# Cross keys of two sequences in one pass, and a new order of round 0, in a fused decoder layer

## The chip, the cores and the metric

The kernel runs on one core of one Trainium2 chip. The metric is device time in microseconds; three runs of the kernel before took 3400.95, 3402.79 and 3403.72 us, and the median, 3402.79, is the time before. A core has five engines that run side by side, each in the order of its own queue: TensorE (PE in the profile, its weight loads PEld), VectorE (DVE), ScalarE (ACT), GpSimd (POOL) and SyncE (SP), which here only issues DMAs.

## The reference

One decoder layer over 32 sequences of 256 tokens with 256 features, in f32: self-attention with a latent of 72 (16 heads), cross-attention with 16 heads of 64 to a context of 120 rows, and a mixture of 16 experts that each choose 32 tokens of a sequence, with a shared expert beside them. A layernorm follows each part.

```python
# self-attention: one latent serves as keys and as values of all heads
Wdkv = x @ latent_w + latent_b
q = jnp.einsum('btc,hcl->bhtl', x, Wd_w) + Wd_b[None, :, None, :]
scores = jnp.einsum('bhtl,bsl->bhts', q, Wdkv) / np.sqrt(d_head)      # causal mask
y = jnp.einsum('bhts,bsl->bhtl', softmax(scores), Wdkv)
x = _layernorm(x + y_of_all_heads @ out_w + out_b)
# cross-attention: keys and values come from the context alone
k = jnp.einsum('bsd,dhk->bshk', ctx, Wk)
v = jnp.einsum('bsd,dhk->bshk', ctx, Wv)
logits = jnp.einsum('bthk,bfhk->bhft', k, q * depth ** -0.5)
x = _layernorm(x + einsum(softmax(logits), v) @ Wo)
# experts: the 32 best tokens of each expert and sequence
scores = jax.nn.softmax(x @ gate_w.T, axis=-1).transpose(0, 2, 1)
topk_w, topk_idx = jax.lax.top_k(scores, 32)
x = _layernorm(x + scattered(expert(x[topk_idx]) * topk_w) + shared(x))
```

## The kernel before

The kernel has two stages. In the first, which takes about two thirds of the time, a round n (a first and a second half) does the self-attention of sequence n, and beside it later steps of earlier sequences: the self-attention's end and the cross queries of n-1, the cross-attention of n-1 and n-2, and turn_x2, routing and selection of n-3. In the second stage the experts run, one after the other, over 16 sequences each.

The order of TensorE and ACT is written out by hand: the calls in `first_half` and `second_half` are their queues, round after round. In round 0 SP's order is by hand too, and in the opening, up to the call of `load_weights([(wk_sb, wk)])` (lines 959 to 975), that of all engines. In the other rounds a scheduler places the work of VectorE, POOL and SP; it honours `urgent()`, which raises the priority of the copies that empty PSUM. The kernel uses eight banks of PSUM, six of them in one rotation (tag "r"): a step that takes a bank waits until its tenant of six steps ago was copied out.

The steps that matter here:

- `keys` (L342) makes kT on ACT and kD on VectorE from xT. `place_keys` sends kT to kr by four DMAs. `queries(s, g)` (L388) makes the queries of four heads, with eight passes of TensorE over 256 columns and a pair of copies on ACT. `query_rest` makes q8 for the last eight latent columns of all heads. `scores(s, g)` (L416) needs kr, q8, kT, kD and the queries, fills four banks, and VectorE adds the mask.
- `weights(s, g, t)` is the softmax of one block: VectorE takes the maximum, ACT does four exponentials with their sums, VectorE the reciprocals and POOL the product (L471). `turns(s, g)` transposes the result on TensorE (pT), and ACT and VectorE copy it to pt. `weigh`, `weigh_rest` and `latent_out` finish the self-attention, which gives x1; `turn_x1` transposes x1 and VectorE copies the result to x1T, which `cross_queries` needs.
- `load_context(s)` (L330) loads the context of one sequence. `cross_keys(s, n)` (L557) makes one half of its keys: four chunks of 128 features, each with two weight blocks of 128 by 128 against the 120 context rows, into one bank (pkx), and a copy on ACT to kxT. `cross_values` (L571) makes half of the values, pvx to vx. `cross_scores`, `cross_weights` (xsm on ACT, L463, and rs_x on VectorE), `cross_turn` (pxT to xpt), `cross_weigh` and `cross_out` finish the cross-attention.
- In the opening `first_weights` issues the first loads, `order_first` brings the first query weights into order on VectorE (wd_sb, after wdbs), `order_others` the rest on VectorE and POOL. `warm_up(n)` runs n matmuls on a unit matrix whose result nobody reads.
- `select(g)` transposes the scores of eight sequences and copies them to `left`; `choose(g, k)`, for k from 0 to 3, finds the next eight best on VectorE (max, its indices, and a replacement of what was found); `place(g)` turns the indices for the gathers. Select comes at the end of rounds 10, 18 and 26, and `best_of` calls the choose steps in the next round.

Of the kernel before, what the change touches and what calls it, by code (L numbers as in the profile page):

```python
# [32 lines left out]
def decoder_kernel(  # L33
# [208 lines left out]
    def first_weights():  # L242


        nc.sync.dma_start(
            out=lat_sb[:, :, 0:L], in_=latent_w.rearrange("(c p) l -> p c l", p=P)
        )
        by_part = wd_w.rearrange("(c p) n -> p c n", p=P)
        for part in (slice(0, HG * L), slice(HG * L, H * L)):
            nc.sync.dma_start(out=raw[:, :, part], in_=by_part[:, :, part])  # L250
        nc.scalar.dma_start(out=latb[0:L], in_=latent_b.unsqueeze(1))
        for j in range(1, HG):
            nc.scalar.dma_start(
                out=latb[LM + j * LR : LM + (j + 1) * LR], in_=latent_b[LM:].unsqueeze(1)
            )
        nc.scalar.dma_start(out=wdb_sb, in_=wd_b)

        nc.scalar.activation(warm, mhalf[:, 0:1], AF.Exp)
        by_column = wd_b[LM:, :].rearrange("l (g j o) -> j (l g) o", j=HG, o=1)
        for j in range(HG):  # L260
            nc.sync.dma_start(
                out=wdbs[j * 32 : (j + 1) * 32, ZC - 1 : ZC], in_=by_column[j]
            )
        nc.vector.tensor_copy(
            lat_sb[:, :, L:].rearrange("p c (j l) -> p c j l", l=LR),
            lat_sb[:, :, LM:L].unsqueeze(2).to_broadcast([P, DC, HG - 1, LR]),
        )
        nc.sync.dma_start(out=outb, in_=out_b.partition_broadcast(P))

    def pack(copy, g):  # L270
# [46 lines left out]


    states = [{} for _ in range(B)]

# [6 lines left out]
        st["x"] = sp.tile([P, TC, C], F32, tag="x", name=f"x_{s}")  # L327
        nc.sync.dma_start(out=st["x"], in_=x[s].rearrange("(t p) d -> p t d", p=P))

    def load_context(s):  # L330
        st = states[s]
        st["c"] = ap.tile([P, DC, S2], F32, tag="c", bufs=3, name=f"c_{s}")
        nc.sync.dma_start(out=st["c"], in_=ctxT[s].rearrange("(c p) s -> p c s", p=P))

    def turn_x(s):
        st = states[s]
# [217 lines left out]

    def cross_keys(s, n):  # L557
        st = states[s]
        if n == 0:
            st["kxT"] = ap.tile([P, QC, S2], F32, tag="kxT", name=f"kxT_{st['nm']}")  # L560
        pkx = bank("r", [P, 4, S2], f"pkx_{st['nm']}_{n}")
        for c in range(4):
            w0 = (4 * n + c) * P
            project(
                pkx[:, c, :],
                [(wk_sb[:, d, w0 : w0 + P], st["c"][:, d, :]) for d in range(DC)],
            )
        with urgent():
            nc.scalar.copy(st["kxT"][:, 4 * n : 4 * n + 4, :], pkx)

    def cross_values(s, n):  # L571
        st = states[s]
        if n == 0:
            st["vx"] = ap.tile([S2, H, DH], F32, tag="vx", bufs=2, name=f"vx_{st['nm']}")
        pvx = bank("r", [S2, 512], f"pvx_{st['nm']}_{n}")
        project(
            pvx,
            [(st["c"][:, d, :], wv_sb[:, d, n * 512 : (n + 1) * 512]) for d in range(DC)],
        )
# [25 lines left out]
    def cross_scores(s, c0, t):  # L605
        st = states[s]
        nm = f"{st['nm']}_{c0}_{t}"
        pLs = [bank("l", [P, HG, S2], f"pL_{nm}_{odd}") for odd in range(2)]
        for j in range(HG):
            for odd in range(2):  # L610
                rows = slice(odd * DH, (odd + 1) * DH)
                nc.tensor.matmul(  # L612
                    pLs[odd][:, j, :],
                    st["qxT", c0][rows, j, t * P : (t + 1) * P],
                    st["kxT"][rows, c0 + j, :],
                    start=True,
                    stop=True,
                )
        st["pL", c0, t] = pLs
# [127 lines left out]
    def select(g):  # L747

        sc = scs[g]
        pst = bank("r", [P, T], f"pst_{g}")  # L750
        for t in range(TC):
            nc.tensor.transpose(
                pst[:, t * P : (t + 1) * P], sc[:, t].rearrange("p b e -> p (b e)"), ident
            )
        left = ap.tile([P, T], F32, tag="left", bufs=1, name=f"left_{g}")
        with urgent():
            nc.vector.tensor_copy(left, pst)
        idx = ap.tile([P, CAP], mybir.dt.uint32, tag="idx", bufs=1, name=f"idx_{g}")
        ats[g] = left, idx
        choose(g, 0)  # L760

    def choose(g, k):

# [46 lines left out]
    def first_half(n):  # L810
        scores(n, 0)
        run(cross_scores, n - 2, 4, 0)
        run(cross_values, n - 1, 0)
        turns(n - 1, 3)
        both(cross_turn, n - 2, 0, 1)
        both(cross_weights, n - 2, 4, 0)
        queries(n, 1)
        if n == 0:
            turn_x(1)
            keys(1)  # L820
        run(turn_x2, n - 3)
        weights(n, 0, 0)
# [4 lines left out]
            route((n - 3) // BQ)  # L827
        run(cross_weigh, n - 2, 0)
        weights(n, 0, 1)
        best_of(n, 1)  # L830

        scores(n, 1)
        run(cross_scores, n - 2, 4, 1)
        run(latent_out, n - 1)
        if n:
            run(load, n + 1)
            run(load_context, n + 1)
        else:
# [12 lines left out]
        run(cross_weights, n - 2, 4, 1, 1)  # L851
        if n == 0:
            out_weights(0)
        if routed(n):
            score((n - 3) // BQ)
        run(turn_x1, n - 1)
        run(cross_values, n - 1, 1)
        run(cross_queries, n - 1, 0, 0)
        run(cross_queries, n - 1, 0, 2)
        best_of(n, 2)  # L860

    def second_half(n):
# [19 lines left out]
        best_of(n, 3)  # L882

        weigh(n, 0)
        weigh(n, 1)
# [29 lines left out]
    def last_scores():  # L915
# [8 lines left out]
        weights(last, 2, 1)  # L924
        queries(last, 3)
        both(cross_weights, last - 1, 0, 0)
        cross_keys(last, 1)
        scores(last, 3)
        cross_scores(last - 1, 0, 1)
        both(cross_weights, last - 1, 0, 1)  # L930
# [249 lines left out]
    with tc.manual_schedule(engines=pinned):  # L1180
# [43 lines left out]
        score(last // BQ)  # L1224
        fill(3)
        select(B // BG - 1)
        for k in range(1, CAP // 8):
            choose(B // BG - 1, k)
        fill(8)
        place(B // BG - 1)  # L1230
# [54 lines left out]
```

## Time and profile before

| what | value |
|---|---|
| median of three runs | 3402.79 us |
| the profiled execution | 3404.24 us |
| its span, first to last instruction | 3402.5 us |
| VectorE, ACT, POOL busy | 1534.1, 1503.1, 1071.8 us |
| passes over the cross keys (pkx) | 1024 of 128x120 |
| copies to kxT on ACT | 64 of 128x480, median 587 ns |
| passes over the cross values (pvx) | 256 of 120x512 |
| step of a round in the middle of the first stage | 72.96 us (round 3 to 4, from transposes at 211.09 to 284.05) |

The span counts from the first to the last instruction of the profiled execution; what lies around it is 1.7 us. A matmul of f32 data shows in the trace as two passes. Passes are pipelined: the length of a single one (say 274 ns) reaches beyond the start of the next, so a pass's cost is the step from one start to the next, which one reads from a group's length in the chain of waits. An arrow in the column of idle time names what ended a wait.

### The profile page before, as it was taken

What the parts mean: (1) busy time and instruction counts of PE and PEld (TensorE: products, weight loads), DVE (VectorE), ACT (ScalarE), POOL (GpSimd) and SP (SyncE); (2) the same over time, 40 slices, a digit from 0 to 9 for tenths busy, and PEclk for the clock granted to TensorE, in tenths of its full rate; (3) what the DMA queues carried; (4) which work ended last, traced back from release to release, by engine and by line L of the source; (5) the groups of instructions that cost most, each with busy time, mean ns of one, the idle gap of its engine ahead of it and who ended that gap; (6) DMA issues with size and microseconds to landing.
All of it is one profiled execution on the core that took longest, in us unless ns stands there. A gap on an engine that the chain in (4) does not pass through costs nothing.

```text
span 3402.5 us, 60296 instructions
## 1 busy us (share of the span) xinstructions
PE 3379.7 (99%) x23544; PEld 2574.4 (76%) x23544; DVE 1534.1 (45%) x3416; ACT 1503.1 (44%) x5461; POOL 1071.8 (31%) x947
## 2 busy tenths in 40 slices
PE   9999999999999999999999999999999999999999
PEld 7888888888888888888888888887666655666655
DVE  4555555555555555555555555554312133211133
ACT  4655555555555555555555555554311111111111
POOL 3333332323232323233233233233444401444400
PEclk9999999999999999999999999999999999999999
DMA  3000000000000000000000000003455531555421
GB/s 99 9 17 23 20 21 18 18 18 23 20 17 22 17 18 18 26 17 20 19 18 17 24 20 20 17 12 102 112 122 122 137 90 57 124 123 122 105 86 47
DMA packets 142883, 164.56 MB, mean 48 GB/s; under 512 B 29448, under 2 KB 118536, under 8 KB 142600
## 3 DMA queue, kind: packets, MB, share of 16 engines
q1 hardware_dynamic: 117808, 126.08, 12.4%
q0 software_dynamic: 24576, 34.62, 5.8%
q8 instruction: 187, 3.06, 0.4%
q14 instruction: 96, 0.79, 0.1%
q10 hardware_dynamic: 216, 0.01, 0.0%
HBM read 105.61 MB, written 50.86 MB: 46 GB/s over the span
## 4 chain that ended last, share of the span: by engine, by line
PE 97%; DVE 1%; ACT 1%; POOL 0%; DMA 0%; issue 0%; POOLq 0%; ACTq 0%
PE po L188 14%; PE pq L188 7%; PE pqx L188 7%; PE pd L188 6%; PE pu L188 6%; PE pg L188 6%; PE pS L438 5%; PE pz L505 5%; PE pT L485 5%; PE pc L654 3%; PE pL L612 3%; PE pkx L188 3%; PE pu_s L188 3%; PE pg_s L188 3%; PE pxT L638 3%; PE pfo L188 3%
## 5 line engine op out<-in xcount | busy, mean ns | idle before, releaser
L471 POOL TENSOR_TENSOR sm<-sm,rs 128x512 f32<-128x512 f32 (+1 forms) x256 | 375.8, 1468 | 457.3 <-DVE rs L470 443.0
L463 ACT ACTIVATE sm<-sm,nmax 128x128 f32<-128x128 f32 (+1 forms) x1024 | 453.5, 462 | 89.5 <-DVE nmax L460 89.5
L471 POOL TENSOR_TENSOR xsm_x<-xsm_x,rs_x 128x480 f32<-128x480 f32 x256 | 252.5, 988 | 733.2 <-DVE rs_x L470 731.2
L463 ACT ACTIVATE xsm_x<-pL,nmax_x 128x120 f32<-128x120 f32 x1024 | 355.6, 378 | 10.5 <-DVE mv L160 7.7
L1059 POOL DMA_INDIRECT acc<-eo,offs x128 | 200.8, 1569 | 335.7 <-DVE eo L1056 294.6
L447 DVE TENSOR_TENSOR sm<-pS,mask 128x384 f32<-128x384 f32 x512 | 248.9, 547 | 90.7 <-PE pS L438 90.6
L188 PE MATMUL pq<-xT,wd_sb 128*128 128x256 f32 x1152 | 279.4, 384 | 0.6 <-DVE wdbs L290 0.6
L188 PE MATMUL po<-ow_sb,zT 128*128 128x256 f32 x1152 | 257.2, 382 | 0.0
L188 PE MATMUL pg<-xeT,wg 128*128 128x512 f32 x512 | 240.8, 593 | 0.0
L188 PE MATMUL pu<-xeT,wu 128*128 128x512 f32 x512 | 240.7, 592 | 0.0
L188 PEld LDWEIGHTS po<-ow_sb,zT 128*128 128x128 f32 x1152 | 216.2, 190 | 31.9
L188 PE MATMUL pqx<-x1T,wq_sb 128*128 128x256 f32 x1024 | 239.7, 382 | 0.0
L1130 DVE TENSOR_TENSOR hT<-gl,pu 128x512 f32<-128x512 f32 x128 | 87.9, 688 | 333.4 <-PE pu L188 199.4
L188 PEld LDWEIGHTS pq<-xT,wd_sb 128*128 128x128 f32 x1152 | 212.2, 191 | 30.5 <-DVE wdbs L290 0.7
L460 DVE TENSOR_REDUCE nmax<-sm 128x4 f32<-128x512 f32 (+1 forms) x256 | 231.4, 945 | 2.3
L463 ACT ACTIVATION_READ_ACCUMULATOR xsm_x<-pL,nmax_x 128x1 f32 x1024 | 229.1, 224 | 0.0
L188 PE MATMUL po<-wo_sb,cxT 128*128 128x256 f32 x1024 | 227.6, 380 | 0.0
L188 PE MATMUL pd<-wd,hT 128*128 128x256 f32 x1024 | 226.6, 379 | 0.0
L188 PEld LDWEIGHTS pqx<-x1T,wq_sb 128*128 128x128 f32 x1024 | 189.6, 190 | 40.7 <-issue 13.6
L470 DVE RECIPROCAL rs<-rs 128x4 f32<-128x4 f32 x256 | 45.5, 178 | 378.1 <-ACT sm L463 374.8
L463 ACT ACTIVATION_READ_ACCUMULATOR sm<-sm,nmax 128x1 f32 x1024 | 211.7, 207 | 0.0
L188 PEld LDWEIGHTS pd<-wd,hT 128*128 128x128 f32 x1024 | 192.1, 190 | 25.7 <-issue 1.0
(139 smaller groups left out, 6075.8 us busy)
## 6 DMA issues: line engine op xcount, KB each, us to landing
wg<-in_wg_dram SPq DMA_DIRECT2D x32, 512.0 KB
wu<-in_wu_dram SPq DMA_DIRECT2D x32, 512.0 KB
wd<-in_wd_dram SPq DMA_DIRECT2D x32, 512.0 KB
x<-in_x_dram SPq DMA_DIRECT2D x32, 256.0 KB
rows<-x SPq DMA_DIRECT2D x32, 256.0 KB
acc<-x SPq DMA_DIRECT2D x32, 256.0 KB
x2t<-x2T SPq DMA_DIRECT2D x32, 256.0 KB
fx2T_s<-x2t SPq DMA_DIRECT2D x16, 512.0 KB
```

The lines of the kernel that those rows point to most:

```text
L188: nc.tensor.matmul(acc, lhsT, rhs, start=(i == 0), stop=(i == n - 1))
L438: nc.tensor.matmul(pS[2 * a + odd][:, SEG[t]], st["qT", g][rows, a, t * P : (t + 1) * P], k[rows, 0 : (t + 1) * P], start=False, stop=(t = ...
L447: nc.vector.tensor_tensor(sm[:, j, :], pS[j], mask, ALU.add)
L460: nc.vector.tensor_reduce(nmax, src, AX.X, ALU.max, negate=True)
L463: nc.scalar.activation(dst[:, a, :], src[:, a, :], AF.Exp, bias=nmax[:, a : a + 1], accum_out=rs[:, a, :],)
L471: nc.gpsimd.tensor_tensor(dst, dst, rs.to_broadcast([P, n, width]), ALU.mult)
L485: nc.tensor.transpose(pT[:, j, :], block, ident)
L505: nc.tensor.matmul(pz[odd * LM : (odd + 1) * LM, a, k * P :], st["v"][:, k, 0:LM], moving(st, g, 2 * a + odd, k), start=(k == 0), stop=(k ...
L612: nc.tensor.matmul(pLs[odd][:, j, :], st["qxT", c0][rows, j, t * P : (t + 1) * P], st["kxT"][rows, c0 + j, :], start=True, stop=True,)
L638: nc.tensor.transpose(pT[:, j, :], st["xsm", c0, t, odd][:, j, :], ident)
L654: nc.tensor.matmul(pc[odd * DH : (odd + 1) * DH, a, :], st["vx"][:, 2 * (c0 + j0 + a) + odd, :], st["xpt", c0, odd][:, j0 + a, :], start=True,
L1059: nc.gpsimd.indirect_dma_start(out=acc[b], out_offset=self.rows(b), in_=eo[:, k, :], in_offset=None, compute_op=ALU.add,)
```

## The change

1. `cross_keys` works on a pair of sequences. A context tile holds both sequences side by side, so each weight block meets 240 columns in one pass. A half of the keys now takes two banks of two chunks, and two copies to kxT. The tile of the keys is one for each half, with one buffer each, in place of two buffers for the whole. Pairs from the second on do this in odd rounds: the first half of the keys in the first half of the round, the second in the second. In even rounds `cross_keys` is left out. Pair 0 is done in round 0.
2. `load_context` loads a pair, by two DMAs, in even rounds, in place of one sequence in each round.
3. In the opening `order_first` comes ahead of `keys(0)`, the first queries directly behind the first keys, `warm_up(6)` goes, and the context loads move behind `wk`. `load(1)` moves ahead of `outb`.
4. In rounds 0 and 1 `queries(0, 2)`, `queries(0, 3)` and `queries(1, 1)` stand earlier, and the pair's keys stand where `queries(0, 2)` stood.
5. In every round `both(cross_turn, n - 2, 4, 0)` moves from ahead of `queries(n, 2)` to behind `turn_x1`. In even rounds `cross_values(n - 1, 1)` takes the place that `cross_keys` leaves, ahead of `turn_x1`; in odd rounds it stays behind it.
6. `select` no longer calls `choose(g, 0)`; the four choose steps stand one place later each.

```diff
@@ first_weights
+        load(1)
         nc.sync.dma_start(out=outb, in_=out_b.partition_broadcast(P))
@@
-    def load_context(s):
-        st = states[s]
-        st["c"] = ap.tile([P, DC, S2], F32, tag="c", bufs=3, name=f"c_{s}")
-        nc.sync.dma_start(out=st["c"], in_=ctxT[s].rearrange("(c p) s -> p c s", p=P))
+    def load_context(m):
+
+        pairs[m] = {"c": ap.tile([P, DC, 2, S2], F32, tag="c", bufs=2, name=f"c_{m}")}
+        both_rows = ctxT[2 * m : 2 * m + 2].rearrange("s (c p) k -> p c s k", p=P)
+        for c in range(DC):
+            nc.sync.dma_start(out=pairs[m]["c"][:, c], in_=both_rows[:, c])
@@
-    def cross_keys(s, n):
-        st = states[s]
-        if n == 0:
-            st["kxT"] = ap.tile([P, QC, S2], F32, tag="kxT", name=f"kxT_{st['nm']}")
-        pkx = bank("r", [P, 4, S2], f"pkx_{st['nm']}_{n}")
-        for c in range(4):
-            w0 = (4 * n + c) * P
-            project(
-                pkx[:, c, :],
-                [(wk_sb[:, d, w0 : w0 + P], st["c"][:, d, :]) for d in range(DC)],
-            )
-        with urgent():
-            nc.scalar.copy(st["kxT"][:, 4 * n : 4 * n + 4, :], pkx)
+    def cross_keys(m, n):
+
+        pair = pairs[m]
+        kxT = ap.tile([P, 4, 2, S2], F32, tag=f"kxT{n}", bufs=1, name=f"kxT_{m}_{n}")
+        pair["kxT", 4 * n] = kxT
+        for c in range(0, 4, 2):
+            pkx = bank("r", [P, 2, 2 * S2], f"pkx_{m}_{n}_{c}")
+            for a in range(2):
+                w0 = (4 * n + c + a) * P
+                project(
+                    pkx[:, a, :],
+                    [
+                        (
+                            wk_sb[:, d, w0 : w0 + P],
+                            pair["c"][:, d].rearrange("p s k -> p (s k)"),
+                        )
+                        for d in range(DC)
+                    ],
+                )
+            with urgent():
+                nc.scalar.copy(kxT[:, c : c + 2].rearrange("p a s k -> p a (s k)"), pkx)
...
@@ select
-        choose(g, 0)
@@ first_half
         run(cross_values, n - 1, 0)
+        if n == 1:
+            queries(1, 1)
         turns(n - 1, 3)
...
-        queries(n, 1)
+        if n != 1:
+            queries(n, 1)
         if n == 0:
             turn_x(1)
+            queries(0, 2)
             keys(1)
...
-        best_of(n, 1)
+        best_of(n, 0)
...
             run(load, n + 1)
-            run(load_context, n + 1)
         else:
             query_rest(1)
-            queries(0, 2)
+            cross_keys(0, 0)
             turns(0, 0)
...
-        both(cross_turn, n - 2, 4, 0)
         if n:
             queries(n, 2)
         run(cross_weights, n - 2, 4, 1, 0)
-        cross_keys(n, 0)
+        if n % 2 and n > 1:
+            cross_keys(n // 2, 0)
+        else:
+            run(cross_values, n - 1, 1)
         run(cross_weights, n - 2, 4, 1, 1)
...
         run(turn_x1, n - 1)
-        run(cross_values, n - 1, 1)
+        both(cross_turn, n - 2, 4, 0)
+        if n % 2 and n > 1:
+            run(cross_values, n - 1, 1)
+        if n % 2 == 0 and 2 <= n < B - 2:
+            load_context(n // 2 + 1)
         run(cross_queries, n - 1, 0, 0)
         run(cross_queries, n - 1, 0, 2)
-        best_of(n, 2)
+        best_of(n, 1)
@@ second_half
         run(cross_queries, n - 1, 4, 0)
+        if n == 0:
+            queries(n, 3)
         turns(n, 1)
...
-        queries(n, 3)
         if n:
+            queries(n, 3)
             run(keys, n + 1)
...
-        best_of(n, 3)
+        best_of(n, 2)
...
-        cross_keys(n, 1)
+        if n % 2 and n > 1 or n == 0:
+            cross_keys(n // 2, 1)
+        best_of(n, 3)
         weights(n, 3, 0)
...
@@ opening
         first_weights()
-        load_context(0)
-        load(1)
-        load_context(1)
         turn_x(0)
+        order_first()
         warm_up(3)
         keys(0)
-        warm_up(6)
+        queries(0, 0)
         place_keys(0)
-        order_first()
-        queries(0, 0)
         order_others()
         query_rest(0)
         values(0)
         load_weights([(wk_sb, wk)])
+        load_context(0)
+        load_context(1)
```

`cross_values` and `cross_scores` read the pair's tiles in place of the sequence's own.

More of the change, by code (lines that the diff above doesn't have):

```diff
@@ L319, in decoder_kernel @@
     states = [{} for _ in range(B)]
+    pairs = [{} for _ in range(B // 2)]
     def load(s):
@@ L553, in turn_x1 @@
         transposed(st["x1T"], st["x1"], f"px1T_{st['nm']}")
-    def cross_keys(s, n):
-        st = states[s]
-        if n == 0:
-            st["kxT"] = ap.tile([P, QC, S2], F32, tag="kxT", name=f"kxT_{st['nm']}")
-        pkx = bank("r", [P, 4, S2], f"pkx_{st['nm']}_{n}")
-        for c in range(4):
-            w0 = (4 * n + c) * P
-            project(
-                pkx[:, c, :],
-                [(wk_sb[:, d, w0 : w0 + P], st["c"][:, d, :]) for d in range(DC)],
-            )
-        with urgent():
-            nc.scalar.copy(st["kxT"][:, 4 * n : 4 * n + 4, :], pkx)
+    def cross_keys(m, n):
[18 more added lines that the diff above has]
+                nc.scalar.copy(kxT[:, c : c + 2].rearrange("p a s k -> p a (s k)"), pkx)
     def cross_values(s, n):
         st = states[s]
+        c = pairs[s // 2]["c"][:, :, s % 2, :]
         if n == 0:
@@ L577, in cross_values @@
             pvx,
-            [(st["c"][:, d, :], wv_sb[:, d, n * 512 : (n + 1) * 512]) for d in range(DC)],
+            [(c[:, d, :], wv_sb[:, d, n * 512 : (n + 1) * 512]) for d in range(DC)],
         )
@@ L614, in cross_scores @@
                     st["qxT", c0][rows, j, t * P : (t + 1) * P],
-                    st["kxT"][rows, c0 + j, :],
+                    pairs[s // 2]["kxT", c0][rows, j, s % 2, :],
                     start=True,
@@ L926, in last_scores @@
         both(cross_weights, last - 1, 0, 0)
-        cross_keys(last, 1)
+        cross_keys(last // 2, 1)
         scores(last, 3)
@@ L1226, in decoder_kernel @@
         select(B // BG - 1)
-        for k in range(1, CAP // 8):
+        for k in range(CAP // 8):
             choose(B // BG - 1, k)
```

## The prediction

> **What bounds the kernel now.** I read the page's first part, the TensorE groups by shape, the waits of TensorE, and then the chain of waits and the timeline where something moves.
>
> ```profile
> PE 3379.7 (99%) x23544; PEld 2574.4 (76%) x23544; DVE 1534.1 (45%) x3416; ACT 1503.1 (44%) x5461; POOL 1071.8 (31%) x947
> L188 PE MATMUL pkx<-c,wk_sb 128*128 128x120 f32 x1024 | 124.3, 274 | 0.0
> PE pT L485 <- POOL sm L471: 5.8, 4, 2.0
> PE pzr L526 <- DVE pt L489: 4.4, 3, 1.5
> PE pk L188 <- DVE xT L182: 1.5, 1, 1.5
> ```
>
> TensorE is the bound: busy 3379.7 of 3402.5 us, nothing else above half. So a change pays only where it removes TensorE time or one of TensorE's few waits. The second row is the group the change rewrites, 512 matmuls that the trace shows as two passes each. A mean of 274 ns is not a cost, since passes overlap; the cost is the step from pass to pass, which the chain of waits shows:
>
> ```profile
> 45.51 1.79 PE pkx L188 x16
> ...
> 73.59 1.73 PE pq L188 x8
> 75.32 1.78 PE pkx L188 x16
> ...
> 77.53 1.72 PE pvx L188 x4
> ```
>
> The columns are start, length, engine, tile, passes. A pass over 120 columns costs 1.783/16 = 111.4 ns, over 256 columns 1.73/8 = 216.2, over 512 1.72/4 = 430. From 256 to 512 that is 0.835 ns a column, so 120 columns alone would be some 103: here something else, the load of 128 weight columns, holds the step at 111.4.
>
> **Part 1, keys for two sequences in a pass.** Removed: 1024 passes of 120 columns, 114.1 us. Added: 512 passes of 240 columns. No row has 240, the nearest is 256: 216.2 - 16 x 0.835 = 202.8 ns, so 103.8 us. Bounds: 200 by the line through zero, 216 if 256 is charged; 102.4 to 110.6. One pair goes from 4 x 1.783 = 7.13 to 6.49: **0.64 us a pair**, 9.6 for pairs 1 to 15 (pair 0 is in part 2). The Trainium skill, TensorE: Matmul & The Clock Gate, section Back-to-back issue gap, says that a step is N/2.4 + 2.5 ns. By it 240 columns take 102.5, the weight load would bind, and halving the passes would save half of 114, some 57 us. The rows give twice the page's slope for this f32 data; I take the rows.
>
> The copies to kxT stay 64 of 128x480 on ACT, the context loads 32 issues of the same bytes on SP; each is needed over a round later. kxT falls from two buffers to one of each half; in the written order the last reads of the pair before stand over half a round ahead of the new writes, so no wait.
>
> **Part 2, the start** (up to the fourth transposes of sequence 1). I follow the chain with durations of before. Keys 0 end at 7.4. The first queries came at 9.29, behind VectorE's pack of wd_sb (8.81 to 9.24), which stood behind kD (7.94). Now the pack stands ahead of kD: its data landed at 5.9 (semaphore records), so it is done at 6.6, and the queries run 7.3 to 9.1. The six removed warm-ups (12 passes, 7.24 to 8.74) filled that wait and cost nothing. Query_rest needs wdbs, whose last load lands at 8.84, and two packs of 0.25: 9.45 to 10.3. ACT's q then ends at 11.0 (0.47 each). kr is issued at 7.95 instead of 9.08, as three context loads left SP's queue ahead of it, and lands by some 10.5 behind x_1 and outb. **First scores: 12.76 becomes 11.05.**
>
> Masks and two reductions (1.95 and 1.81) hold xT_1 on VectorE until 6.2 us after the first scores; the wait of 1.5 in the rows above is that. Queries(0, 2), 1.73, now fill it: keys 1 at 17.3 (19.03). ACT's first exponentials start at 18.8 (20.54), POOL's product ends at 24.6 (26.33). Scores, query_rest and now pkx with 3.24 reach the first turns at 24.7 instead of 25.13 with a wait: no wait. But ACT does two key copies and two pt copies (0.59 each) before the exponentials of group 1: these start at 26.8 (27.99), and POOL releases the second turns at 32.65 (33.85). TensorE waits about 2.1 there, 1.64 before. As queries 3 are already done, weigh follows at 33.6 (36.67). The third turns come without a wait; pkx ends at 45.0, ACT's copies behind it let the fourth exponentials start at 45.6 (47.78), POOL ends at 51.4. Queries(1, 1), now ahead of those turns, fill most of the wait of 1.5. **weigh_rest: 52.3 instead of 56.45, 4.1 gained.**
>
> Round 1 has no pkx. Before x1T there is now no work between turn_x1 and the cross queries: x1T lands 1.06 us after the last turn, 0.95 of it a wait, against 1.78 saved. Its second pkx hid behind a wait that stays: the fourth turns of sequence 1 waited 2.03 at 114.48 for exponentials at 108.60. These lose only the key copy ahead of them, 0.44. So at 114.48 **5.4 us are gained** (4.1 + 1.78 - 0.95 + 0.44). This chain could be off by 2.5 either way.
>
> That wait has a price of its own:
>
> ```profile
> 112.40:115.80 3.40, 1.37 (x13) 1.32 (x13) 3.40 (x7) 0.99 (x3) 1.90 (x1) 1.00 0.00 0
> 115.90:119.20 3.30, 3.30 (x12) 2.80 (x10) 1.21 (x3) 2.59 (x13) 0.00 (x0) 0.50 0.00 0
> ```
>
> The third number from the end is the granted clock: after 2.03 us of waiting TensorE ran at half clock for 3.4 us, about 1.7 lost. The same page of the skill (Part 1) wants an idle window of some 3.4 us before the clock halves; the row shows that less suffices, and the waits of 1.5 and 1.64 did not trip it. By the page the longer wait after the change (some 3.4, in two pieces) would be the first to cost 1.7; by the row it is paid already, so the sum changes by 0. The wait of 2.1 at 32 could trip it newly: 0 to 1.7, I take 0, for it is nearest to 1.64.
>
> **Part 3, rounds 2 to 31, what the moves uncover.** In even rounds the filler pkx is gone, and pvx moves ahead of turn_x1; the two cross turns (0.87 together) stand behind it. In the round shown:
>
> ```profile
> 213.28 1.89 PE L188 MATMUL pq<-xT,wd_sb 128*128 128x256 f32 x8
> ...
> 215.21 0.84 ACT L403 ACTIVATE qT<-pq,wdbs 128x256 f32<-128x256 f32 x2 [1.09 <-PE pq L188]
> ...
> 217.45 0.18 DVE L470 RECIPROCAL rs_x<-rs_x 128x4 f32<-128x4 f32 x1 [1.74 <-ACT xsm_x L463]
> 217.54 0.66 DVE L182 COPY x1T<-px1T 128x512 f32<-128x512 f32 x1
> ...
> 218.94 1.24 PE L188 MATMUL pqx<-x1T,wq_sb 128*128 128x256 f32 x5
> ```
>
> VectorE's copy x1T stands behind rs_x, which waits for eight ACT instructions behind qT, which waits for pq. Counted from the end of pq (215.17), x1T ends at +3.03 and pqx could start at +3.1; today pvx covers that (pqx at +3.77). In the changed program's order the same queue stands (x1, rs_x, x1T, then xpt). TensorE now reaches pqx at -0.17 + 1.72 (pvx) + 0.44 + 0.87 = +2.86. So **0.24 us of waiting in each of 15 even rounds, 3.6 lost**; between 0, if TensorE's own steps are a little longer, and 0.4. In odd rounds pvx stays in front of pqx, no wait. x1 itself is ready: turn_x1 comes 0.94 earlier, and x1 was 1.07 early with xpt (0.66) still in its queue, which leaves it.
>
> Without the second pkx TensorE reaches the fourth turns 1.78 earlier in even rounds. POOL's product ends at 257.00 and the turn that needs it starts at 261.69, a slack of 4.69; ACT starts 0.44 earlier, 3.35 stay: no cost. In odd rounds ACT is 0.55 later, TensorE 1.46: no cost.
>
> **Part 4, selection later.** The three waits of pzr (4.4 us) are VectorE's max, find and replace (0.42 each) ahead of a pt copy, in rounds 11, 19 and 27. VectorE's order is the scheduler's, and in the built program the instructions from left to at stand in exactly the old places. Cost and gain 0. If the call's place decided, 4.4 would go. The last selection runs in the same order too.
>
> **Sum**: 5.4 + 9.6 - 3.6 = 11.4 us. The profiled execution took 3404.24 (span 3402.5); I expect a span of 3391.1. The median of before is 3402.79, so **3391.4**. What a measurement here can tell from no change is 0.2%, 6.8 us.
>
> **The rivals.**
> A. The small waits don't come: x1T is in time (+3.6), or the selection waits go after all (+4.4). For it: 0.24 is a difference of two sums with five terms. 3387. Chance 0.20.
> B. The start gives nothing lasting, because ACT sets it: the waits at 32, 51 and 114 grow as TensorE gets ahead, and the half clock falls once more. 9.6 - 3.6 + 1 to 2 leave 7 to 8 less 1.7: 3397. For it: four of the waits of before are POOL's products behind ACT. Against: their chain begins with the first scores, which come earlier. Chance 0.12.
> C. Slower: the x1T wait of even rounds is much larger. If x1T is in effect behind the second rs_x too (ACT's vx copy 0.59 and a second group of exponentials 1.53), the wait is 2.4 us, 36 in 15 rounds: 3402.8 - 15.0 + 36 = 3424. It decides from 1.0 us a round; the built order has that rs_x behind x1T, so 0.04.
> D. The pass of 240 columns costs as 256 or the pairing does less: -6.7 on the forecast, 3398. Chance 0.04.
> The forecast has 0.60 (3389 to 3395). The range 3385 to 3397 takes in A and the better part of B and leaves C and most of D out. Faster by over 0.2% (below 3396.0): the forecast, A and a third of B, 0.84; within 0.2%: the rest of B and D, 0.12; slower 0.04.
>
> **What would show it.** pkx: 512 passes, 3.24 us for 16 in the chain. First scores at 11, weigh_rest at 52. A wait of pqx for x1T, fifteen times 0.2 and once 0.9. The waits of pzr still three times 1.5. Wrong would be: a pass of 240 columns far from 203, no wait for x1T or one near 2 us, a wait of the fourth turns in later rounds.

## The result and the profile after

| | before | after |
|---|---|---|
| median of runs, us | 3401.98 | 3393.84 |
| range of runs, us | 3400.95 to 3403.72 | 3391.95 to 3398.84 (15 runs) |
| profiled execution, us (span) | 3404.24 (3402.5) | 3392.11 (3390.3) |

The ratio of the times is 0.9977, its 95% interval 0.9969 to 0.9985: the changed kernel is 8 us, 0.24%, faster. The forecast was 3391.4, a gain of 11.4. The runs of after lie wider than those of before, over 6.9 us instead of 2.8.

From the page's first part, then the passes over the cross keys, and then the waits of TensorE (engine, tile, line, what it waited for, us in total, times, longest):

```profile
PE 3368.9 (99%) x23020; PEld 2558.0 (75%) x23020; DVE 1538.1 (45%) x3416; ACT 1502.3 (44%) x5461; POOL 1070.3 (32%) x947
```
```profile
L188 PE MATMUL pkx<-c,wk_sb x512: 365/366/369, 21.6 to 2282.1; 128*128 128x240 f32 x171
```
```profile
PE pzr L530 <- DVE pt L493: 4.4, 3, 1.5
PE pT L489 <- POOL sm L475: 3.7, 2, 2.1
...
PE pqx L188 <- ACT vx L594: 0.8, 1, 0.8
PE pq L188 <- DVE wd_sb L295: 0.5, 1, 0.5
```

TensorE stays the bound and is 10.8 us less busy. The three waits of pzr are what they were, as forecast. Two of the four waits of pT for POOL's products are gone, and so is that of keys 1 for xT. The 0.8 put down to ACT's vx is the wait for x1T in round 1, which has the order of the even rounds: vx was done 0.64 us before pqx started. The last row is new and looks harmless: query_rest, the last four passes of pq at the start, waits 0.5 us for a pack of VectorE.

The chain of waits of after, in the rows that answer to the forecast's steps (start, length, engine, tile, passes):

```profile
5.22 3.47 DMA wdbs<-in_wd_b_dram
...
9.20 0.71 PE pq L188 x2
...
10.95 0.94 PE pS L430 x16
...
17.48 0.86 PE pk L188 x4
...
21.78 3.24 PE pkx L188 x16
...
32.70 1.09 PE pT L489 x8
...
52.84 2.74 PE pzr L530 x64
...
74.69 3.69 PE pqx L188 x16
...
109.70 1.09 PE pT L489 x8
```

| step | forecast | measured |
|---|---|---|
| 16 passes of pkx | 3.24 | 3.24 |
| first scores | 11.05 | 10.95 |
| keys 1 | 17.3 | 17.3 (the chain's row begins where the pass before ends) |
| second turns | 32.65, wait 2.1 | 32.70, wait 1.64 |
| weigh_rest | 52.3 | 52.8 |
| wait of pqx in round 1 | 0.95 | 0.83 |
| fourth turns of sequence 1 | 109.1 (5.4 gained) | 109.70 (4.8 gained) |
| from there to the end of the span | 6.0 gained | 5.7 gained, see below |

The last row takes out one effect. In the profile of before TensorE ran at half clock from 115.9 to 119.2 us, which costs about 1.7; in this profile of after it did not, up to its last matmuls. So 3402.5 - 114.48 - 1.7 = 3286.3 us remained before, 3390.3 - 109.70 = 3280.6 after. Like for like, the profiles show 4.8 + 5.7 = 10.5 us, against 11.4 in the forecast. The medians of the runs show 8.1 here and 9.4 in e1.

The forecast's wait for x1T in even rounds is there. The timeline of round 16 (start, length, engine, line, operation):

```profile
1161.81 0.60 PE L178 MATMUL px1T<-ident,x 128*128 128x128 f32 x4
...
1162.53 0.18 DVE L474 RECIPROCAL rs_x<-rs_x 128x4 f32<-128x4 f32 x1 [1.31 <-ACT xsm_x L467]
1162.63 0.66 DVE L182 COPY x1T<-px1T 128x512 f32<-128x512 f32 x1
...
1163.34 0.48 PE L188 MATMUL pqx<-x1T,wq_sb 128*128 128x256 f32 x1
```

The turns end at 1162.41, and VectorE is idle; but rs_x, which waits for ACT until 1162.53, stands ahead of x1T in its queue, and x1T starts at 1162.63. Here and in the other even rounds without routing pqx starts 1.21 us after the last px1T pass was issued, where TensorE's own steps take 0.98: 0.23 lost. In even rounds with routing it is 1.28, and 0.30 lost. Over 8 rounds of the one kind and 7 of the other that is 3.9 us; 3.6 was forecast.

### The profile page after: what moved, and what is told of

Same layout as the page of the kernel before. It is cut to its first block, busy times and chain, and to the rows that moved or that the text cites. A ratio compares the mean times of both kernels' runs of the same rounds, so it can differ in the third digit from the quotient of the medians.

```text
span 3390.3 us, 59258 instructions
## 1 busy us (share of the span) xinstructions
PE 3368.9 (99%) x23020; PEld 2558.0 (75%) x23020; DVE 1538.1 (45%) x3416; ACT 1502.3 (44%) x5461; POOL 1070.3 (32%) x947
## 4 chain that ended last, share of the span: by engine, by line
PE 96%; DVE 2%; ACT 2%; POOL 0%; issue 0%; DMA 0%; SPq 0%; POOLq 0%; DVEq 0%; ACTq 0%
PE po L188 13%; PE pq L188 7%; PE pqx L188 7%; PE pd L188 7%; PE pu L188 6%; PE pg L188 6%; PE pS L442 5%; PE pz L509 5%; PE pT L489 5%; PE pc L667 3%; PE pu_s L188 3%; PE pg_s L188 3%; PE pL L625 3%; PE pfo L188 3%; PE pS L430 3%; PE pkx L188 3%
## 5 line engine op out<-in xcount | busy, mean ns | idle before, releaser
L467 ACT ACTIVATE xsm_x<-pL,nmax_x 128x120 f32<-128x120 f32 x1024 | 354.3, 375 | 13.2 <-DVE mv L160 10.2
```

Source lines behind the costliest of these rows:

```text
L467: nc.scalar.activation(dst[:, a, :], src[:, a, :], AF.Exp, bias=nmax[:, a : a + 1], accum_out=rs[:, a, :],)
```

## Experiments

Times are compared with the runs of the kernel before on the same chip in the same batch: its medians were 3402.86 for e1, e2, e3 and e5, 3403.84 for e4, e4b, e6 and e8b, 3403.76 for e9 to e11, and 3402.31 for e12. So gains of two batches can be compared, but only roughly. The edits are shown against the changed kernel, with three dots where lines are left out.

**e1. The changed kernel again**, for more runs and a second profile.

> The changed kernel as it is. Its fifteen times lie in steps (3392, 3394, 3395.5, 3397, 3399), and the runs with a lower mean clock are the longer ones. Clock theory: a time is 3392 plus 1.7 us for each stretch of 3.4 us at half clock, so a run of 3397 has three of them, and its mean clock is 0.998. Rival (transfers or other engines differ from run to run): times spread as much at a mean clock of 1.000.

Measured: 3393.43 (3392.22 to 3397.25, 10 runs), 9.4 below before, ratio 0.9974 (0.9965 to 0.9984). The runs stand in steps: five at 3392.2 to 3392.7, four at 3394.1 to 3395.0, one at 3397.25. The profiled run took 3394.14, and its trace shows why. These are stretches of 3.41 us: length, busy time (and instructions) of PE, PEld, DVE, ACT and POOL, then the granted clock, DMA share and GB/s.

```profile
106.80:110.21 3.41, 1.33 (x8) 0.68 (x7) 2.55 (x6) 1.88 (x6) 2.26 (x2) 1.00 0.02 5
110.21:113.62 3.41, 3.41 (x17) 3.36 (x16) 1.93 (x3) 0.73 (x2) 0.00 (x0) 0.50 0.00 0
```

The wait at the fourth turns, 2.08 us up to 109.96, lies whole in the first stretch; in the next TensorE is busy throughout at clock 0.50. From 109.96 to the end this run took 1.7 us longer than the profile of after from 109.70. The same wait in the first profile of after:

```profile
104.51:107.92 3.41, 3.10 (x20) 1.56 (x16) 2.11 (x7) 3.41 (x16) 1.95 (x3) 1.00 0.00 0
107.92:111.33 3.41, 1.63 (x15) 1.63 (x16) 3.24 (x6) 0.99 (x3) 1.73 (x1) 1.00 0.02 5
111.33:114.75 3.42, 3.42 (x48) 2.60 (x49) 0.81 (x2) 3.13 (x17) 0.69 (x1) 1.00 0.00 0
```

The wait has the same length, 2.10, but a border of the stretches cuts it into 0.32 and 1.78, and the clock stays. The stretches are not chosen freely: in every profile here the clock changes only at whole multiples of 3.413 us after the instant at which it first rose, and that instant lay anywhere from 4.97 to 7.86 us. In the two profiles of this one program it was 5.52 and 7.81. So whether one and the same wait costs 1.7 us is a matter of phase, which differs from execution to execution. It makes 1.7 of the 2.0 us between the two profiled runs, 3392.11 and 3394.14; that the other runs of the first two steps differ by it too is likely, not shown. The recorded mean clocks fit the expectation for the long runs: it is 0.998 for the four of after from 3396.77 on and for 3397.25 here, 0.999 or 1.000 for all others of the two. They are too coarse to count stretches.

The phase also moves the start of a profile: the first scores came at 10.95 in after and at 11.21 here, so 0.3 us between the starts of two profiles says nothing.

**e2. The pairs alone**: the old opening and the old order of rounds 0 and 1, pair keys from the change.

```diff
         if n == 0:
             turn_x(1)
-            queries(0, 2)
             keys(1)
...
             query_rest(1)
-            cross_keys(0, 0)
+            queries(0, 2)
             turns(0, 0)
...
-        if n % 2 and n > 1:
+        if n % 2 and n > 1 or n == 0:
             cross_keys(n // 2, 0)
...
+        load_context(0)
+        load(1)
+        load_context(1)
...
         keys(0)
-        queries(0, 0)
+        warm_up(6)
         place_keys(0)
+        order_first()
+        queries(0, 0)
```

> Pairs, with the rounds as in the changed kernel, but the opening and the order of rounds 0 and 1 of before. Theory (pairs give 0.64 us each, the x1T wait of even rounds takes back 3.9): span 3397, a gain of 5; the first scores at 12.8 as before. Rival (the start gives nothing, all comes from pairs): span near 3391, as the changed kernel.

Measured: 3398.73 (3397.64 to 3399.46, 13 runs), 4.1 below before, ratio 0.999 (0.9982 to 0.9998). Its fourth turns come at 115.22, 0.7 later than before (0.45 of that is there at the first scores already), and 3395.9 - 115.22 = 3280.7 us remain, as in after. So the rounds gain 5.7 with or without the new opening, and no gain of pair 0 shows in the old one. The runs lie within 1.8 us.

**e3. The start alone**: the new opening and the new order of rounds 0 and 1; cross keys, context loads and selection as before (the old functions, which the edit below leaves out, came back too).

```diff
-        if n % 2 and n > 1:
-            cross_keys(n // 2, 0)
-        else:
-            run(cross_values, n - 1, 1)
+        if n:
+            cross_keys(n, 0)
...
+        both(cross_turn, n - 2, 4, 0)
...
-        both(cross_turn, n - 2, 4, 0)
...
-        if n % 2 and n > 1 or n == 0:
-            cross_keys(n // 2, 1)
+        cross_keys(n, 1)
```

> The new opening and the new order of rounds 0 and 1, with keys for one sequence at a time in every round as before. Theory: about 5.9 us at the fourth transposes of sequence 1 and nothing after, span 3396.6, no wait of pqx for x1T in later rounds. Rival (the start gives nothing lasting): span 3402. If the missing warm-up matmuls make the clock fall, times spread here by 5 us or more, as in the changed kernel; if the wait of two microseconds before the fourth transposes does it, they spread too, and the second half of pair 0 in round 1 tells the two apart.

Measured: 3397.71 (3395.9 to 3402.68, 13 runs), 5.2 below before, ratio 0.9987 (0.9979 to 0.9995). The two halves add up: 4.1 + 5.2 = 9.3, and e1 in the same batch has 9.4. The start gives over half of the gain, so rival B is out. And one run of 13 lies about 5 us above the median here, none of 13 in e2: a first sign that the long runs belong to the opening, not to the pairs.

**e5. The second half of pair 0's keys in round 1.** In after it stands in round 0; the wait at the fourth turns of sequence 1 then has nothing ahead of it.

```diff
-        if n % 2 and n > 1 or n == 0:
+        if n % 2:
             cross_keys(n // 2, 1)
```

> The changed kernel with the second half of pair 0's keys in round 1 instead of round 0. Theory: the fourth exponentials of sequence 0 no longer queue behind the key copies, 3.2 us earlier; in round 1 the keys fill the wait of 2.1 before the fourth transposes, ACT's key copies give back about 1.2: span 3388.3, a wait there of under 1 us. Clock theory with this wait as the cause: the times lie within 2 us of each other, median 3390. Rival (the opening without warm-ups is the cause): the spread of 5 to 7 us stays.

Measured: 3390.74 (3390.4 to 3392.51, 6 runs), 12.1 below before, ratio 0.9967 (0.9955 to 0.9979); 2.7 better than e1. The wait at the fourth turns is 0.47 at 108.40. The forecast had noted that the old second pkx "hid behind a wait that stays"; the change took the cover away and left the wait. The six runs lie within 2.1 us, as expected if this wait made the long runs; but six are few, and e8b has a long run without it.

**e4. Values behind the turns in even rounds too**, which is the order of odd rounds: pvx then covers x1T, but the turns of x1 come 1.7 us earlier.

```diff
         if n % 2 and n > 1:
             cross_keys(n // 2, 0)
-        else:
-            run(cross_values, n - 1, 1)
...
-        if n % 2 and n > 1:
-            run(cross_values, n - 1, 1)
+        run(cross_values, n - 1, 1)
```

> The changed kernel, but in even rounds too the second cross values stand behind turn_x1 and the cross turns. Theory: the wait of pqx for x1T (0.23 to 0.30 in 15 rounds, 3.9) goes, but turn_x1 now comes 1.72 us earlier and x1 was ready only 0.59 ahead of it: a wait of about 1.1 for x1 in each of 15 even rounds, span 3403, slower than the changed kernel by 13. Rival (the filler's place does not matter, only the x1T wait): span 3386.

Measured: 3405.2 (3403.3 to 3410.27, 12 runs), 1.4 above before and not told apart from it, ratio 1.0006 (0.9997 to 1.0014). From its waits of TensorE:

```profile
PE px1T L178 <- DVE x L164: 11.1, 16, 0.8
```

The small wait for x1T is gone (pqx at +2.70 behind pvx, TensorE's own pace) and a larger one stands before it: the turns wait for x1, 0.79 us in plain even rounds and 0.57 in routed ones (1.1 was expected), and behind the wait their four passes start over 0.51 us instead of 0.33. So moving pvx ahead is what makes the pairing pay.

**e4b. Two exponentials ahead of the queries**: ACT's second group of them then ends earlier, and with it rs_x, which holds VectorE in front of x1T.

```diff
+        run(cross_weights, n - 2, 4, 1, 0)
         if n:
             queries(n, 2)
-        run(cross_weights, n - 2, 4, 1, 0)
```

> The changed kernel with the first group of exponentials, cross_weights(n - 2, 4, 1, 0), ahead of queries(n, 2) on ACT. Theory (rs_x stands in front of x1T on VectorE and waits for these exponentials, which wait for the queries): rs_x comes 1.5 us earlier, the pause between the cross turns and pqx shrinks from 0.23 to about 0.08 in unrouted even rounds, 1.2 to 1.5 us in all, span 3389. Rival (x1T is late for itself): no pause changes, span 3390.3.

Measured: 3392.01 (3391.48 to 3396.9, 5 runs), 11.8 below before, ratio 0.9968 (0.9955 to 0.9982). pqx starts 1.06 us after the last turn in plain rounds (1.21 in after) and 1.23 in routed ones (1.28). Over 8 and 7 rounds that is 1.6 us; the medians of e1 and e4b are too coarse to show it. Half a miss: in plain rounds rs_x no longer stands in the way, as expected, and the copy behind the turns sets the time, 0.08 above TensorE's own pace; in routed rounds something else keeps VectorE, and the span was 3391.5 where 3389 was expected, with one stretch at half clock in it.

**e6. Selection in the next round**, before best_of(n, 0): the forecast had said that the call's place decides nothing.

```diff
+        if n - 3 >= BG and (n - 3) % BG == 0:
+            select((n - 3) // BG - 1)
...
-        if n - 3 >= 0 and (n - 2) % BG == 0:
-            select((n - 3) // BG)
```

> The changed kernel with select itself called in the first half of the next round, behind cross_weigh, so that left cannot be filled before. Theory (the scheduler puts the choose steps directly behind left, wherever they are called; only left's place counts): the three waits of weigh_rest for pt (1.45 each) go, 4.4 us, span 3386. Rival (the choose steps then delay another copy): waits of over 1 us of another step in rounds 11, 19 and 27. Clock: if these three waits are what puts runs at 3397, no run of this kernel is over 1.7 us (one stretch) above its fastest, because the wait of 2.1 before the fourth transposes of sequence 1 is left alone.

Measured: 3390.61 (3389.21 to 3392.7, 5 runs), 13.2 below before, ratio 0.9962 (0.9949 to 0.9976); 3.8 more than e1 gained. From its waits of TensorE, where the row of pzr for pt is gone and the others stand:

```profile
PE pT L489 <- POOL sm L475: 3.7, 2, 2.1
...
PE pq L188 <- DVE wd_sb L295: 1.2, 1, 1.2
```

From the fourth turns to the end this profile is 3.1 us shorter than after's; the three waits made 4.4. By 2305 us 4.1 are gained, and 1.0 is lost again behind that, in the part with the last selection, which was not followed further. Its fourth turns come 1.2 later than in after, because of the load behind the second row: it landed 1.2 later here, in code that is the same. Moving the call by a few lines gives nothing; moving it to another round gives the 4 us. The runs lie 3.5 us apart, where the expectation allowed 1.7 if the three waits made the long runs: a first sign against them.

**e8b. e5, e4b and e6 together.**

> The changed kernel with three edits together: the second half of pair 0's keys in round 1, select in the next round, the exponentials ahead of queries(n, 2). Theory: the gains add, 1.7 + 4.4 + 1.3, span 3383, and the times lie within 1.7 us of each other, as no wait of over a microsecond is left behind the first 35 us. Rival (the waits move elsewhere): span over 3386, or times that spread by 5 us.

Measured: 3385.85, 3385.98, 3386.11, 3386.69 and 3390.9, median 17.7 below before, ratio 0.9948 (0.9935 to 0.9962). The profiled run is the long one, and it has 0.47 us of waiting at the fourth turns and none of the selection. Its start, TensorE's timeline and then the stretches:

```profile
7.63 1.03 PE L188 MATMUL pq<-xT,wd_sb 128*128 128x256 f32 x4
11.39 1.18 PE L188 MATMUL pq<-xT,wd_sb 128*128 128x256 f32 x4 [2.74 <-DVE wd_sb L295]
```
```profile
8.92:12.34 3.42, 0.95 (x4) 0.82 (x5) 0.50 (x3) 0.61 (x2) 0.90 (x2) 1.00 0.13 38
12.34:15.75 3.41, 3.04 (x23) 2.38 (x23) 0.42 (x2) 0.47 (x1) 2.18 (x4) 0.50 0.82 239
15.75:19.16 3.41, 3.41 (x18) 2.70 (x15) 2.41 (x5) 0.00 (x0) 0.00 (x0) 0.50 1.11 307
```

The harmless row of 0.5 us has become 2.74, and two stretches at half clock follow. Behind it stands the load at the head of the chain: 

```profile
5.22 5.67 DMA wdbs<-in_wd_b_dram
```

The fourth of the small loads into wdbs (some 100 bytes) was issued at the same 5.22 as in after and landed 5.67 us later instead of 3.47. The records of its landing show 15 of its 16 parts by 8.65 and the last at 10.88; in after all had landed by 8.69, in e6 by 9.88. VectorE waits for it to scale one column of wdbs, and the two packs for query_rest, which don't need it, stand behind that in VectorE's queue.

The small load was not slow by itself. All four small loads have one late part, at 10.25, 10.46, 10.67 and 10.88, and so has the load issued ahead of them, the second part of the query weights (ow_sb): 15 parts by 7.96, the last at 10.04. One packet of that load, 3456 bytes, took 1.70 us from 5.89, where the median of its kind is 0.135. The records don't name the engine of a packet, but all this fits one engine that fell behind there and took the small loads in turn. In e6 a packet of 0.78 us goes with a landing at 9.88 in the same way. Why a packet is slow is open.

At this point there were two explanations of the long runs. *Start*: the load lands late. *Selection*: the three waits of 1.45 us of rounds 11, 19 and 27 are 587.15 us apart in after, almost exactly 172 stretches, so they could halve the clock all three together. e9 to e12 tell them apart.

**e9. The small loads later** by 0.9 us.

```diff
+        load(1)
+        nc.sync.dma_start(out=outb, in_=out_b.partition_broadcast(P))
         by_column = wd_b[LM:, :].rearrange("l (g j o) -> j (l g) o", j=HG, o=1)
...
-        load(1)
-        nc.sync.dma_start(out=outb, in_=out_b.partition_broadcast(P))
```

> The changed kernel, with the loads of x_1 and outb (384 KB) ahead of the four small wdbs loads in SP's queue instead of behind them; they are issued 0.9 us later. In the changed kernel query_rest of round 0 starts 0.5 us after these loads have landed, and waited 0.54 us in one profile, 1.0, 1.2 and 2.7 us in those of three of its variants; in the last TensorE then ran at half clock for 6.8 us, and that execution was 4.8 us above the others. Theory (start): the spread of the changed kernel, 3392 to 3398.8, is these loads, which end when the last of 16 DMA engines has written its part. Then all runs shift by about 1 us and most of them also lose one or two stretches at half clock, 1.7 or 3.4 us: median 3396 to 3399, the wait in the profile 1.4 us or more. Rival (selection): the long runs come from the three waits of 1.45 us in rounds 11, 19 and 27: the median moves by the 1 us alone, to 3394.5, and the share of runs 4 to 5 us above the fastest stays a quarter.

Measured: 3396.98 (3394.88 to 3399.92, 16 runs), 6.8 below before, ratio 0.9982 (0.9974 to 0.9989). The four small loads were issued 0.9 us later and the last landed at 9.71; that costs 2.6 us of the 9.4 in e1 (two batches, and the intervals overlap), where *selection* expected 1. In its profile the wait is 2.02 us, and one stretch at half clock follows:

```profile
9.08:12.50 3.42, 1.42 (x6) 0.88 (x6) 1.68 (x5) 0.93 (x3) 3.17 (x5) 1.00 0.41 99
12.50:15.91 3.41, 3.33 (x26) 2.87 (x28) 0.18 (x2) 0.00 (x0) 0.00 (x0) 0.50 1.07 369
```

**e10. The small loads on ACT's queue, and the packs ahead of the scaling.** (ACT's first activation moved behind the loads, too.)

```diff
-            nc.sync.dma_start(
+            nc.scalar.dma_start(
                 out=wdbs[j * 32 : (j + 1) * 32, ZC - 1 : ZC], in_=by_column[j]
...
 def order_others():
-        nc.vector.tensor_scalar(
-            wdbs[:, ZC - 1 : ZC], wdbs[:, ZC - 1 : ZC], QSCALE, None, ALU.mult
-        )
         for d in range(DC):
             nc.vector.tensor_copy(...)
+        nc.vector.tensor_scalar(
+            wdbs[:, ZC - 1 : ZC], wdbs[:, ZC - 1 : ZC], QSCALE, None, ALU.mult
+        )
```

> The changed kernel, with the four wdbs loads on ACT's queue, issued from 2.8 us on instead of 3.9, not behind the 1.2 MB of down weights, and with VectorE's two packs for query_rest ahead of its scaling of wdbs. Theory (start): query_rest follows the queries with no wait, first scores at 10.5 instead of 10.95, and the runs at 3397 to 3399 are gone: all between 3391 and 3394, in the two steps that the wait of 2.1 us at the fourth transposes makes (with and without one stretch at half clock, 1.7 us); median 3392. Rival (selection): the three waits of 1.45 us stay, so a quarter of the runs stays 4 to 5 us above the fastest; median 3393.

**e12. e10 once more.**

> The kernel of e10 once more, for more runs. Of 71 runs of the kernels with the new opening and the old place of the four wdbs loads, 9 were 4 us or more above the fastest of their kernel; of the 11 runs of e10 and e11 none was, which a share of 9 in 71 would also give one time in five. Theory (start): again no run 4 us above the fastest, 3392 to 3395.5. Rival (the long runs come from the three selection waits of 1.45 us, which this kernel keeps): one run in four to one in eight at 3397 or above.

Measured: e10 3392.97 (3392.21 to 3395.13, 6 runs), 10.8 below before, ratio 0.9968 (0.9956 to 0.998); e12 3392.07 (3391.31 to 3394.04, 7 runs), 10.2 below before, ratio 0.997 (0.9959 to 0.9981). No run of the 13 lies 4 us above the fastest of its kernel, with the selection waits (1.45, three times) in place. In e10's own profile the first queries run through, but so they do in e1, where the clock also rose late (7.86 and 7.81) and TensorE reached query_rest late. The clearer case is e11 (below), which has the same opening: its clock rose at 5.20, its queries begin as early as in after (6.77), and query_rest follows without a wait:

```profile
6.75 2.94 PE L188 MATMUL pq<-xT,wd_sb 128*128 128x256 f32 x12
```

No run separates the two edits, but the traces leave only the order of the packs: on ACT's queue the loads were issued at 3.9 to 5.2, as before (2.8 was expected), and landed no earlier (their scaling started at 9.09 in e11 and 9.42 in e10 and e12), but query_rest doesn't wait for them now: in e11 its first pass starts at 8.55, and the scaling only at 9.09. No late load was caught in these three profiles, so that the new order bears one is argued, not seen. The median gained only about 1 us on e1: in e12 the first scores waited 1.06 us for kr, which is late next.

**e11. e8b with the edits of e10.**

> The same two edits in the kernel with the three edits of e8b (second half of the first pair's keys in round 1, selection in the next round, exponentials ahead of the queries). e8b's runs were 3385.9, 3386.0, 3386.1, 3386.7 and, with a wait of 2.7 us and 6.8 us at half clock in the start, 3390.9. Theory (start): first scores 0.4 us earlier, no run above 3387.5, median 3385.6. Rival (selection or another cause): one run in five stays near 3390.9, since nothing else in this kernel's start is changed.

Measured: 3385.68 (3385.01 to 3385.73, 5 runs), 18.1 below before, ratio 0.9946 (0.9933 to 0.996). All runs lie within 0.7 us. It is the best version found: about twice the gain of the change. Its only waits of TensorE over 1 us are the first identity and the second turns (1.6 of the first row):

```profile
PE pT L489 <- POOL sm L475: 2.1, 2, 1.6
PE cold L126 <- POOL ident masks.py:199: 1.7, 1, 1.7
PE pqx L188 <- ACT vx L594: 0.8, 1, 0.8
```

What stays open. That all long runs are the late load is not shown: only one was profiled. A count over all runs of the kernels with the new opening and the old place of the loads (after, e1, e3, e4, e4b, e5, e6, e8b) gives 11 of 71 at 4 us or more above the fastest of their kernel (the expectation of e12 says 9; it missed two of e4). At that rate the 18 runs of e10, e11 and e12 would show none about one time in twenty. Nine of the 11 have a recorded mean clock of 0.998 and none of the other 60 has, so lost clock is part of the long runs; what started the loss in the others is open. More direct evidence against the selection waits: one of 1.45 us leaves a stretch of 3.41 at least 57% busy, and in no profile was a stretch at full clock and over 42% busy followed by half clock (see the last section).

## Why the prediction was right, and where it was short

The direction and the order of size held: 3391.4 forecast, 3393.84 and 3393.43 measured. As gains, 11.4 was forecast, 8.1 and 9.4 came. That the first profile's span, 3390.3, lies nearer to the 3391.1 forecast is luck in part: no stretch at half clock fell on that execution.

- **Pairs, 9.6 us and the slope of f32 passes: right.** The trace shows 3.24/16 = 202.5 ns a pass for 202.8. Had the slope of the Trainium skill held (TensorE: Matmul & The Clock Gate, Back-to-back issue gap: N/2.4 + 2.5 ns, given for the gap of a single matmul, without a data type), the change would have gained, as an estimate, some 47 us more. Rival D is out. That the weight load held the old step of 111.4 ns fits the profile of before, where PEld was busy 121.9 us in this group with 1.7 idle; no run tests it.
- **x1T in even rounds: right in mechanism, slightly short.** 0.23 and 0.30 a round, 3.9 in all, for 3.6. e4 shows that the other order loses the whole gain. Rival A is out, as both waits came, and so is rival C, as no wait is near 1 us.
- **Fourth turns without a cost in later rounds: right.** In most rounds their slack is 3.37 us behind an even round (3.35 forecast) and 5.71 behind an odd one; the least is 3.01.
- **Selection, 0: right.** The three waits stand; e6 shows what moves them.
- **Start: the mechanism was right, its size 0.6 too high in the profile.** 4.8 instead of 5.4: weigh_rest was 0.5 later than worked out, and that is nearly all of it. (A wait of 0.36 at 104.03 for ACT's cross exponentials was not foreseen, but cost nothing, since TensorE waits again at the fourth turns.) e3 bears out that the opening is worth 5 us.
- **The half clock, "the sum changes by 0": not settled by the wait's length.** The forecast took the stretch at 115.9 as "paid already". e1 shows that it is paid in some executions and not in others. For the medians 0 was a fair value, since the wait is about as long as before (2.10 for 2.03); for the two profiles compared above it was 1.7. The wait at the second turns was 1.64, not 2.1, and tripped nothing.
- **The weak step: "Query_rest needs wdbs, whose last load lands at 8.84".** It was taken as a fixed time, and query_rest at 9.45 as its consequence. Before the change the first queries held TensorE until 11.0, so that a load landing at 10 would have cost nothing. The change brings the queries forward to 6.8 and removes that cover, and with it the warm-ups that kept TensorE busy. Landings in the profiles here go from 8.7 to 10.9; the wait was 0.54 in after, 1.0 in e5, 1.2 in e6 and 2.7 in e8b, and none in e1 and e4b, where the clock rose only at 7.8 and 7.5 and the queries came later. A wait of 2 can halve the clock for one or two stretches on top (e9, e8b). Of the 2.0 to 3.3 us of gain that are missing, 0.9 is in the start and in x1T, by like-for-like profiles. The remaining 1 to 2.4 is of the size that e10 and e12 gain on e1 and after (0.8 to 2.7 by their distance to before), but the medians are too coarse to prove the share.

## What to carry to other kernels

When work is pulled forward at the start of a kernel, ask of each operand how late it may land, not when it landed in one profile: a load whose wait is 0.5 us in the trace has no slack left, and its spread goes into the time. In a hand-ordered queue, put what needs only early data ahead of what waits for a late load, even where one profile shows no gain. A small load is as late as what stands ahead of it. And where a filler is taken from in front of a wait, the filler's cost comes back as the wait: move it to the place that waits instead (e5), and move a burst on a side engine to another round rather than by a few lines (e6).

## What the hardware showed that was not expected

In all profiles here half clock follows from how busy TensorE was in one stretch of a fixed grid of 3.413 us. The Trainium skill, TensorE: Matmul & The Clock Gate, Part 1, describes such a free-running window; the traces agree with the grid, but not with its rule that an idle window is needed. Stretches at full clock on both sides of the border:

| profile | PE busy in the stretch of 3.41 us | next stretch |
|---|---|---|
| e8b, start | 0.95 | half clock, two stretches |
| e4b, e10, fourth turns | 1.32 | half clock |
| e1, fourth turns | 1.33 | half clock |
| e3, fourth turns | 1.38 | half clock |
| e9, start | 1.42 | half clock |
| after, last matmuls (from 3381.31) | 1.49 | full |
| e2, fourth turns | 1.57 | full |
| after, fourth turns | 1.63 | full |
| e6, fourth turns | 1.63 | full |

The border lies between 1.42 and 1.49 us busy, 42 to 44% of the stretch (1.57 and 46% if the last matmuls, whose ends are modelled, are left aside). So a wait of just under 2 us is enough where it falls whole into one stretch, and one of 2.1 goes free where a border cuts it. A wait of 1.45 to 1.64 us never did it.

A load of some 100 bytes can have its last part 2.2 us behind the other fifteen (8.65 and 10.88 in e8b), and its consumer waits for the last. The delay came from ahead of it: a single packet of 1.70 us in the weight load before it, with a median of 0.135.
